# Spreading a side product over the first attention head of a graph network: earlier start, a split made in halves, and casts shared between two engines

## The chip, the cores and the metric

The kernel runs on one core of one Trainium2 chip. The metric is the time of one execution on the device in microseconds (us); lower is better. Three runs of the kernel before gave 1754.12, 1755.75 and 1757.56 us, so its median is 1755.75 us. One further execution was taken by the hardware profiler. The engines are TensorE (PE; its weight loads are listed apart as PEld), VectorE (DVE), ScalarE (ACT), GpSimd (POOL) and SyncE (SP), which only issues transfers here. ScalarE issues some transfers too.

## The reference: what is computed

Four residual layers of a graph network act on x (2708 nodes, 512 features) and one adjacency matrix of zeros and ones. Each takes h = relu(layernorm(x)) and adds its result to x. Layer 2, in which the change lies, is attention with 8 heads of 64 features:

```
Wh   = h @ W[head]                         # 2708 x 64
e    = leaky_relu(f1[n] + f2[m], 0.2)      # f1 = Wh . a1,  f2 = Wh . a2
e    = where(adj[n, m] > 0, e, -9e15)
out  = elu(softmax(e, over m) @ Wh)
```

The other layers multiply h with the adjacency (layer 0), with the first 64 neighbours of each node (layer 1), and with the neighbour mean and two dense products (layer 3).

## The kernel before

The nodes are cut into 22 chunks of 128; the last has 20. The layers run one after the other, with the edges of each overlapped: the first chunks of a layer start while the last of the layer before are still being summed. The neighbour pattern is held in SBUF for the whole kernel as uint8 tiles, `vT0` to `vT5`.

**Layer 2, projection stage.** `stages2` runs over the 22 chunks: load, normalize, transpose on TensorE, evict with relu on ScalarE (`hT`, line 247), multiply with all heads' weights (`wh_ps`, line 187), copy to SBUF on ScalarE (`wh`), store to DRAM (`whd`). VectorE and GpSimd multiply with a1 and a2 and reduce (`wh_a`, `f`), which gives `f12`, the values f1 and f2 of every node and head. From `f12` ScalarE makes exponentials: `er` of f1 (`exps_nodes`), `ef` and `ec` of f2 (`exps2`). `row2` turns a chunk of `er` into a row on TensorE, copies it on ScalarE and sends it to DRAM (`rT`), from where `load_row1` spreads it over all partitions (`rb`). In this way exp(leaky_relu(f1 + f2)) becomes the maximum of two products; common factors of a node cancel in the softmax.

**Layer 2, attention.** Work is listed in `steps`: ten units with 22 steps each, one step for each chunk m. The first head is two half-width units (1408 and 1300 columns), heads 1 to 6 are one full-width unit each (2708 columns), and the last head is two halves again. In one step:

- `scale` (line 1042) multiplies the 64 columns of Wh by `ef` on ScalarE, and in some steps also a constant column (`one6`), giving the weights `whs` (four buffers).
- `make` (line 1056) computes on VectorE, in one pass, max(rb, ec) times the pattern: the tile `t` (four buffers).
- `multiply` (line 1274) runs `t` past the weights on TensorE, in four column groups side by side: `av` collects the weighted sums of Wh, `sums` the sum of weights.
- In heads 1 to 6 and for the 17 chunks in `BY_SIDE`, `sums` is not formed from `t`. There `compare` (line 1077) makes a comparison mask on ScalarE by a very steep sigmoid with bias `eb`, and `multiply_sides` multiplies this with `parts`.

`parts` holds `ef` and `ec*ef`, each as three bf16 numbers that add up to the fp32 value. `split` (line 1313) makes them: a ScalarE cast to bf16, a VectorE subtraction giving the remainder (`rest`), and so on; it also makes `eb` and copies the last three parts in another order to `parts2`.

**The neighbour sums.** For heads 1 to 6 the comparison gives only one of two sums; to complete the other the kernel needs, once for all heads, the plain neighbour sum of the `ec*ef` parts. These are the `adj_sums`: 17 sets, one for each chunk in `BY_SIDE`. A set is four casts of a quarter of a pattern row from uint8 to bf16 (`mask`, line 1347, ScalarE, 704 or 650 columns) and eight matmuls with `parts2` (`count_neighbors`, line 1355). The casts go to buffers of the tag "x", of which there are five. They run within the first head, whose `sums` come from `t` and need no mask.

**The last chunk.** Its 20 rows of heads 1 to 6 are packed together as one 120-row tile (`tails_row`, `tails_w`, `tails_f`): `load_tails` issues their transfers, `exp_tails` and `make_tails` compute on them.

**What sets the order.** The loop over `steps` emits, at step s, `scale` and `make` for step s+3, `compare` for s+1, the matmuls for s, and then whatever `behind(step, function, ...)` has planned for s (the `behind` calls start at line 1397). A scheduler then orders each engine's instructions by its own estimate of readiness; `tc.issue_after(ins)` holds instructions of an engine behind `ins` if they are on the same engine. `made` lists the VectorE instruction of each step's `t`. The engines work through their lists in order, and semaphores carry data between them.

Of the kernel before, what the change touches and what calls it, by code (L numbers as in the profile page):

```python
# [8 lines left out]
F32 = mybir.dt.float32  # L9
F32R = mybir.dt.float32r  # L10
BF16 = mybir.dt.bfloat16
# [3 lines left out]
AF = mybir.ActivationFunctionType  # L15
ALU = mybir.AluOpType
# [4 lines left out]
P = 128  # L21

R = 128
# [21 lines left out]
def fast_layers(  # L45
# [36 lines left out]
    nc = tc.nc  # L82
    N, D = x_in.shape
    H, _, O = w2.shape
    NC = -(-N // R)
# [6 lines left out]
    def rows(c):  # L92
        return min(R, N - c * R)
# [18 lines left out]
    EARLY = NC // 2  # L112
# [10 lines left out]
    common = ctx.enter_context(tc.tile_pool(name="common", bufs=2))  # L123
# [146 lines left out]
    def dense(src, product_of, twice=True, more=(), scalar=False, rows_of=natural):  # L270

        kept = {}

        def size(c):
            return R if twice else rows(c)

        def load(c):
            kept[c] = load_x(src, c, twice=twice, rows_of=rows_of)

        def normalize(c):  # L280
            kept[c] = kept[c], norm(kept[c], size(c), scalar)

        def transpose(c):
            kept[c] = kept[c][0], relu_T(kept[c][1], size(c))

        def multiply(c):
            product_of(c, *kept.pop(c), size(c))

        return (0, load), (1, normalize), (2, transpose), (3, multiply), *more
# [113 lines left out]
    vT = []  # L403
# [69 lines left out]
    with ExitStack() as ring_ctx:  # L473
# [31 lines left out]
        with tc.tile_pool(name="l0", bufs=2) as wk, ExitStack() as ctx_l0:  # L505
            units = [(g, m) for g in range(len(groups)) for m in range(NC)]
            tiles, acc, sums, xs = {}, {}, {}, {}
# [190 lines left out]
            def first_dense(lag, fn):  # L698
                return lag, lambda i: fn(i) if i < NC else None
# [39 lines left out]
            first = [first_dense(lag, fn) for lag, fn in dense(x_in, product0, rows_of=paired)]  # L739
# [158 lines left out]
        def before1(c):  # L898
# [9 lines left out]
            lambda *args: product2(*args),  # L908
            False,
            [(3, lambda c: save_last2(c)), (4, lambda c: sums2(c)), (6, lambda c: rows2(c))],  # L910
            scalar=True,
        )
# [11 lines left out]
    BY_SIDE = [m for m in range(NC - 1) if m % 5 != 2]  # L924


    STEEP = 2.0**62
    ABOVE = 1.0 + 2.0**-21
# [9 lines left out]
    def in_tails(u, m):  # L938
        return m == NC - 1 and units[u][0] in middle
# [7 lines left out]
    def by_side(u, m):  # L947
        return 1 < u < len(units) - 1 and m in BY_SIDE
# [12 lines left out]
    ef = at.tile([R, NC, H], F32, name="ef")  # L961
    ec = at.tile([R, NC, H], F32, name="ec")
    eb = at.tile([R, NC, H], F32, name="eb")
    parts = at.tile([R, NC * H * 8 + S], BF16, name="parts")
    nc.gpsimd.memset(parts, 0.0)
    parts_of = parts[:, : NC * H * 8].rearrange("p (m h k) -> p m h k", h=H, k=8)

    parts2 = at.tile([R, len(BY_SIDE), 2, H, 3], BF16, name="parts2")
    nc.gpsimd.memset(parts2, 0.0)
    one6 = at.tile([R, S], F32, name="one6")  # L970
    nc.gpsimd.memset(one6, 0.0)
    nc.gpsimd.memset(one6[:, 6:7], 1.0)
    row, weight, wh, whs, acc, sides, made = {}, {}, {}, {}, {}, {}, []

    def load_row1(h, lo, hi):

        if lo == 0:
            row[h] = at.tile([R, N], F32, name="rb", bufs=2)
        src = rT[h : h + 1, lo:hi]
        nc.sync.dma_start(  # L980
            row[h][:, lo:hi],
            bass.AP(tensor=src.tensor, offset=src.offset, ap=[[0, R], [1, hi - lo]]),
        )
# [58 lines left out]
    def scale(s):  # L1042

        u, m = steps[s]
        h, q = units[u][0], rows(m)
        if in_tails(u, m):
            whs[s] = tails_w[:LINES, middle.index(h)]
            return
        t = at.tile([R, O + S], F32, name="whs", bufs=4)
        by = ef[:q, m, h : h + 1]  # L1050
        nc.scalar.activation(t[:q, :O], wh.pop((u, m))[:q], AF.Copy, scale=by)  # L1051
        if not by_side(u, m):
            nc.scalar.activation(t[:q, O:], one6[:q], AF.Copy, scale=by)
        whs[s] = t[:q]

    def make(s):
# [84 lines left out]
    def row2(c):  # L1141
        pf = ps.tile([P, R], F32, name="f_ps", tag="ps")
        nc.tensor.transpose(pf[:H], er[:, c], ident[:R, :R])
        r = at.tile([H, R], F32, name="row", bufs=2)
        nc.scalar.copy(r, pf[:H])
        nc.scalar.dma_start(rT[:, c * R : (c + 1) * R], r)

    def exps_nodes(cs):
        nc.scalar.activation(er[:, cs], f12[:R, cs, :H], AF.Exp, scale=1.0 - SLOPE2)

    def exps2(cs):
        nc.scalar.activation(ef[:, cs], f12[:R, cs, H:], AF.Exp)
        nc.scalar.activation(ec[:, cs], f12[:R, cs, H:], AF.Exp, scale=SLOPE2 - 1.0)


    LATE = NC - 5
    early_rows = [(0, EARLY // 2 + 1), (EARLY // 2 + 1, EARLY)]

    def rows2(c):
        for first, end in early_rows:  # L1160
            if c == end - 1:
                exps_nodes(slice(first, end))
            for n in range(2):
                if first <= first + 2 * (c - end + 1) + n < end and c >= end - 1:
                    row2(first + 2 * (c - end + 1) + n)
        if c == EARLY + 1:
            load_row1(*units[0])

        if c == LATE:
            exps2(slice(0, EARLY))  # L1170
            load_wh(0)
            load_wh(GROUP)
        if LATE < c <= LATE + 3:
            scale(len(made))
            make(len(made))

    def save_last2(c):
# [7 lines left out]
    tails = tails_ctx.enter_context(  # L1185
        tc.tile_pool(name="tails", bufs=1, side="right", reuse_waits="tile")
    )
# [122 lines left out]
                    t[j * step : j * step + height, : b - a],  # L1310
                )

    def split():

        nc.scalar.mul(eb, ec, -STEEP * ABOVE)
        rest = common.tile([P, D], F32, name="rest", tag="t", bufs=3)
        rest = rest[:R, : NC * H].rearrange("p (m h) -> p m h", h=H)
        for i in range(2):
            e = ef
            if i:  # L1320
                nc.vector.tensor_tensor(rest, ec, ef, ALU.mult)
                e = rest
            for k in range(3):
                part = parts_of[:, :, :, 3 * i + k]
                nc.scalar.copy(part, e)
                if k < 2:
                    nc.vector.tensor_tensor(rest, e, part, ALU.subtract)
                    e = rest
        for i, heads in enumerate((slice(1, H), slice(1, H - 1))):
            kinds = sorted({m % 5 for m in BY_SIDE})  # L1330
            for r in kinds:
                ms = [m for m in BY_SIDE if m % 5 == r]
                src = parts_of[:, r : ms[-1] + 1 : 5, heads, 3:6]
                at_i = [BY_SIDE.index(m) for m in ms]
                assert at_i == list(range(at_i[0], at_i[-1] + 1, len(kinds)))
                nc.scalar.copy(
                    parts2[:, at_i[0] : at_i[-1] + 1 : len(kinds), i, heads], src
                )


    fourths = [0, cut // 2, cut, (cut + N) // 2, N]
    counted, masks = [], {}

# [3 lines left out]
    def mask(i, j):  # L1347
        m = BY_SIDE[i]
        q = rows(m)
        g, k = where[m]  # L1350
        own = slice(fourths[j], fourths[j + 1])
        t = masks[i, j] = common.tile([P, D], F32, name="x", bufs=XBUFS).bitcast(BF16)
        nc.scalar.copy(t[:q, : own.stop - own.start], vT[g][:q, k, own])

    def count_neighbors(i):
        m = BY_SIDE[i]
# [37 lines left out]
    def behind(s, fn, *args):  # L1394
        plan.setdefault(s, []).append((fn, args))
# [3 lines left out]
    for c in range(EARLY, NC):  # L1399
        behind(4 + (c - EARLY) // 2, row2, c)  # L1400
    behind(10, load_row1, *units[1])
    behind(9, split)
    behind(12, load_tails)
    behind(18, exp_tails)
    behind(22, make_tails)
    behind(30, load_l3_weights)
    behind(30, spread_nodes)
    for u in range(2, len(units)):
# [3 lines left out]
        behind((u + 1) * NC - 1, evict, u, 0)  # L1412
        behind(min((u + 1) * NC, len(steps) - 1), evict, u, 1)
    for i in range(len(BY_SIDE)):
        first = 11 + 7 * i // 4
        for j in range(4):
            behind(first + j // 2, mask, i, j)
        behind(first + 2, count_neighbors, i)
# [17 lines left out]
    for s in range(len(steps)):  # L1436
        if s == (len(units) - 3) * NC + 1:
            tails_ctx.close()
            e3_ctx = ctx.enter_context(ExitStack())
            e3 = e3_ctx.enter_context(  # L1440
                tc.tile_pool(name="e3", bufs=2, side="right", reuse_waits="tile")
            )
        if s + 6 < len(steps) and (s + 6) % NC % GROUP == 0:
            load_wh(s + 6)
        if s + 3 < len(steps):
            scale(s + 3)
            make(s + 3)
        if s + 1 < len(steps):
            compare(s + 1)
        multiply(s)  # L1450
        multiply_sides(s - 1)
        for fn, args in plan.pop(s, ()):
            if fn in (load_l3_weights, spread_nodes, split):
                with tc.issue_after(made[s]):
                    fn(*args)
            else:
                fn(*args)
# [742 lines left out]
```

## Time and profile before

| | us |
|---|---|
| median of three runs | 1755.75 |
| the profiled execution, whole | 1757.88 |
| its span, from the first to the last instruction | 1756.1 |
| TensorE busy (98% of the span) | 1728.0 |
| VectorE busy (74%) | 1307.0 |
| ScalarE busy (48%) | 850.1 |
| first matmul of the attention | 812.56 |
| first matmul of the second half-unit of head 0 | 872.24 |
| first product of head 1 on VectorE | 907.28 |
| first matmul on the packed tail (end of head 0) | 912.51 |

The clock granted to TensorE was 0.994 in the mean. The shares in the table are averages over stages with different limits. In the projection stage and in the first head TensorE's matmuls carry the chain of work that ended last; from about 1081 us on, VectorE's products `t` carry it up to the end of the attention. In the answers below a line begins with its start and its length in us, or with engine and tile; "x16" is a count of instructions, and "[6.45 <-PE sums L1266]" says that the engine was idle for 6.45 us before and what ended this. One fp32 matmul of the program is two in the trace, and names lose their digits: `t2` of the code is `t`, `parts2` is `parts`, and a cast of the neighbour sums writes `x`.

### The profile page before, as it was taken

To read this page: it belongs to the slowest core of one execution; us is meant where nothing else is said; L and a number is where in the kernel's file an instruction comes from. 1 tells how busy PE (TensorE), PEld (TensorE's weight loads), DVE (VectorE), ACT (ScalarE), POOL (GpSimd) and SP (SyncE) were. 2 spreads that over 40 slices of the span, in tenths; PEclk is the share of its full clock that TensorE was granted. 3 is DMA by queue.
4 is the path that set the end of the run, shared out by engine and by line. 5 is a ranking of instruction groups with operands and counts; after the bars stand their busy time and mean duration, and the time that the engine had idled before them with its cause. 6 is when DMAs were issued, how large, how long until landed. Compare 5 with 4: busy or idle time off the path is not lost.

```text
span 1756.1 us, 29494 instructions
## 1 busy us (share of the span) xinstructions
PE 1728.0 (98%) x11280; PEld 1050.8 (60%) x11280; DVE 1307.0 (74%) x1889; ACT 850.1 (48%) x1547; POOL 248.0 (14%) x252
## 2 busy tenths in 40 slices
PE   8999999999999999999999999999999999999998
PEld 5567777744468887644474554433434455588886
DVE  7759889855455557878699999999999777633334
ACT  5447777622210000365888888888794566400000
POOL 1003323311111112265000000000001222100000
PEclk9999999999999999999899999999999999999999
DMA  8436666444551112332420221122022444313221
GB/s 291 139 117 199 206 207 186 136 114 129 115 135 49 48 49 66 113 126 93 125 63 15 60 64 34 38 64 61 14 68 69 135 139 132 112 34 110 74 72 41
DMA packets 167227, 177.37 MB, mean 101 GB/s; under 512 B 84127, under 2 KB 106591, under 8 KB 166060
## 3 DMA queue, kind: packets, MB, share of 16 engines
q1 hardware_dynamic: 144428, 131.99, 27.1%
q10 hardware_dynamic: 18808, 33.37, 5.1%
q0 software_dynamic: 3840, 10.03, 1.5%
q8 instruction: 90, 1.47, 0.4%
q14 instruction: 61, 0.50, 0.1%
HBM read 111.64 MB, written 55.36 MB: 95 GB/s over the span
## 4 chain that ended last, share of the span: by engine, by line
PE 84%; DVE 9%; issue 2%; ACT 2%; DMA 1%; SPq 0%; POOL 0%; ACTq 0%; DVEq 0%; POOLq 0%
PE acc L424 36%; PE av L1266 15%; PE nb_ps L187 8%; DVE t L1066 6%; PE h_ps L187 4%; PE line_ps L187 4%; PE sums L1266 4%; PE self_ps L187 4%; PE hT_ps L245 2%; PE wh_ps L187 2%; PE fused_ps L370 2%; PE av_ps L1219 1%; PE adj_sums L1365 1%; ACT b L1084 1%; DVE kt L870 0%
## 5 line engine op out<-in xcount | busy, mean ns | idle before, releaser
L1066 DVE SCALAR_TENSOR_TENSOR t<-rb,ec,vT 128x2708 f32<-128x2708 f32 (+2 forms) x214 | 510.7, 2453 | 19.5 <-PE sums L1266 17.8
L1266 PE MATMUL av<-t,whs 128*32 128x451 f32 (+5 forms) x4432 | 431.1, 514 | 4.4 <-DVE t L1066 1.4
L424 PE MATMUL acc<-halves,kt 128*128 128x512 f32 x1848 | 426.4, 391 | 2.4 <-DVE kt L870 2.1
L424 PEld LDWEIGHTS acc<-halves,kt 128*128 128x128 f32 x1848 | 345.2, 188 | 79.8 <-DVE kt L870 6.8
L1084 ACT ACTIVATE b<-t,eb 128x2708 bf16<-128x2708 f32 (+1 forms) x119 | 285.0, 2395 | 36.6 <-DVE t L1066 36.2
L1266 PEld LDWEIGHTS av<-t,whs 128*32 128x32 f32 (+1 forms) x4432 | 168.1, 110 | 182.2 <-issue 145.4
L424 PE MATMUL acc<-halves,ar 128*128 128x512 f32 x924 | 243.6, 414 | 0.0
L424 PEld LDWEIGHTS acc<-halves,ar 128*128 128x128 f32 x924 | 172.6, 188 | 58.2 <-issue 20.8
L223 ACT ACTIVATE ln_rs<-ln_mv,eps 128x1 f32<-128x1 f32 x88 | 25.6, 294 | 306.4 <-DVE ln_mv L221 298.4
L870 DVE SCALAR_TENSOR_TENSOR kt<-lastr,index,vT 128x512 fp32r<-128x512 int16 (+3 forms) x154 | 112.6, 742 | 75.8 <-PE acc L424 75.4
L1517 DVE CAST kt<-vT 128x512 fp32r<-128x512 uint8 (+3 forms) x154 | 56.3, 368 | 131.2 <-PE acc L424 131.2
L1233 POOL TENSOR_SCALAR z<-y 128x512 f32<-128x512 f32 x22 | 44.1, 2003 | 647.1 <-DMA aT<-avT 522.8
L555 DVE TENSOR_TENSOR_SCAN cum<-ai,deg 128x512 int16<-128x512 int32 (+2 forms) x110 | 128.3, 1170 | 0.0
L598 ACT ACTIVATE cum<-cum,limit 128x512 int16<-128x512 int16 (+3 forms) x132 | 88.0, 667 | 51.9 <-DVE deg L563 49.7
L1051 ACT ACTIVATE whs<-wh,ef 128x64 f32<-128x64 f32 x214 | 72.7, 343 | 54.3 <-PE sums L1266 22.0
L219 DVE BATCH_NORM_STATS2 ln_st<-x 128x6 f32<-128x512 f32 x88 | 60.3, 687 | 47.7 <-DMA x<-x 33.3
L1266 PE MATMUL sums<-t,whs 128*32 128x325 f32 (+4 forms) x952 | 92.8, 451 | 0.0
L187 PE MATMUL nb_ps<-wfn,hT 128*128 128x512 f32 x168 | 78.1, 609 | 2.1 <-ACT hT L247 2.1
L187 PE MATMUL h_ps<-w0s,hT 128*128 128x512 f32 x168 | 76.5, 598 | 0.0
L187 PE MATMUL wh_ps<-w2s,hT 128*128 128x512 f32 x168 | 75.9, 594 | 0.3 <-ACT hT L247 0.3
L549 ACT ACTIVATE ar<-ai 128x512 fp32r<-128x512 int32 (+2 forms) x132 | 75.0, 568 | 1.5 <-DMA ai<-in_adj 1.0
L187 PE MATMUL nb_ps<-wn,hT 128*128 128x512 f32 x168 | 75.6, 592 | 0.0
(210 smaller groups left out, 1908.2 us busy)
## 6 DMA issues: line engine op xcount, KB each, us to landing
x<-x SPq DMA_DIRECT2D x105, 256.0 KB
ai<-in_adj SPq DMA_DIRECT2D x84, 256.0 KB
x<-x ACTq DMA_DIRECT2D x84, 256.0 KB
x<-in_x SPq DMA_DIRECT2D x42, 256.0 KB
rb<-rT SPq DMA_DIRECT2D x7, 1354.0 KB
wh<-whd SPq DMA_DIRECT2D x63, 96.0 KB
packed<-two POOLq DMA_DIRECT2D x44, 128.0 KB, 3.2
whd<-wh SPq DMA_DIRECT2D x21, 256.0 KB
```

The lines of the kernel that those rows point to most:

```text
L187: nc.tensor.matmul(po[:n], lhsT[:, f, :n], w[:, f, :], start=(f == 0), stop=(f == NF - 1))
L219: nc.vector.bn_stats(st[:n], xc[:n])
L424: nc.tensor.matmul(acc[:R], weight[:, k * R : (k + 1) * R], parts[:, i, :], start=(m == 0 and i == 0), stop=(m == NC - 1),)
L549: nc.scalar.activation(ar[:, :gw], ai[:, :gw], AF.Square, accum_out=squares[:R, m, g : g + 1])
L555: nc.vector.tensor_tensor_scan(cum[:n, :gw], ai[:n, :gw], ai[:n, :gw], 0.0 if g == 0 else deg[:n, m : m + 1], op0=ALU.add, op1=ALU.max,)
L598: nc.scalar.activation(cum[:n, :gw], cum[:n, :gw], AF.Sign, bias=limit[:n], scale=-1.0, accum_out=signs[:n, m, g : g + 1],)
L870: nc.vector.scalar_tensor_tensor(by_chunk(kt, cs), lastr[:, cs[0] * R : (cs[-1] + 1) * R].rearrange("p (c r) -> p c r", r=R), index[:R, m ...
L1051: nc.scalar.activation(t[:q, :O], wh.pop((u, m))[:q], AF.Copy, scale=by)
L1066: ins = nc.vector.scalar_tensor_tensor(t[:q, : hi - lo], row[h][:q, lo:hi], ec[:q, m, h : h + 1], vT[g][:q, k, lo:hi], op0=ALU.max, op1=AL ...
L1084: nc.scalar.activation(b[:q, : hi - lo], weight[s][:, : hi - lo], AF.Sigmoid, bias=eb[:q, m, h : h + 1], scale=STEEP,)
L1266: nc.tensor.matmul(p[j * S : (j + 1) * S, : b - a], lhsT, rhs[:, part * size + a : part * size + b], start=(s % NC == 0), stop=(s % NC == ...
L1517: nc.vector.tensor_copy(by_chunk(kt, cs), pattern(m, cs))
```

## The change

- The neighbour sums are planned from step 1 on, over 40 steps (`first = 1 + 39 * i // 16`), where before they were planned from step 11 on, over 29.
- `split` becomes a function of a range of chunks. The first half (11 chunks) is made in the projection stage, at its chunk `EARLY + 1`; its exponentials (`exps2`) move up to chunk `EARLY - 1`, from `LATE`. The second half is made at step 9, where the whole was made before.
- Of the last eight sets (chunks from `EARLY` on), the fourth cast runs on VectorE and goes to a new tile `mask` with two buffers in the pool of the tails.
- A cast is held behind the scaling of step s+2 on ScalarE and behind the product of step s on VectorE.
- `exp_tails` moves from step 18 to 30, `make_tails` from 22 to 36.

```diff
+    def split(first, end):
+        cs = slice(first, end)
+        nc.scalar.mul(eb[:, cs], ec[:, cs], -STEEP * ABOVE)
+        rest = common.tile([P, D], F32, name="rest", tag="t", bufs=3)
+        rest = rest[:R, : (end - first) * H].rearrange("p (m h) -> p m h", h=H)
+        for i in range(2):
+            e = ef[:, cs]
+            if i:
+                nc.vector.tensor_tensor(rest, ec[:, cs], e, ALU.mult)
+                e = rest
+            for k in range(3):
+                part = parts_of[:, cs, :, 3 * i + k]
+                nc.scalar.copy(part, e)
+                if k < 2:
+                    nc.vector.tensor_tensor(rest, e, part, ALU.subtract)
+                    e = rest
+        for i, heads in enumerate((slice(1, H), slice(1, H - 1))):
+            kinds = sorted({m % 5 for m in BY_SIDE})
+            for r in kinds:
+                ms = [m for m in BY_SIDE if m % 5 == r and first <= m < end]
...
+                nc.scalar.copy(
+                    parts2[:, at_i[0] : at_i[-1] + 1 : len(kinds), i, heads], src
+                )
...
+        if c == EARLY - 1:
+            exps2(slice(0, EARLY))
         if c == EARLY + 1:
             load_row1(*units[0])
+            split(0, EARLY)

         if c == LATE:
-            exps2(slice(0, EARLY))
             load_wh(0)
...
         own = slice(fourths[j], fourths[j + 1])
+        n = own.stop - own.start
+        if j == 3 and m >= EARLY:
+            t = masks[i, j] = tails.tile([P, fourths[1]], BF16, name="mask", bufs=2)
+            nc.vector.tensor_copy(t[:q, :n], vT[g][:q, k, own])
+            return
         t = masks[i, j] = common.tile([P, D], F32, name="x", bufs=XBUFS).bitcast(BF16)
-        nc.scalar.copy(t[:q, : own.stop - own.start], vT[g][:q, k, own])
+        nc.scalar.copy(t[:q, :n], vT[g][:q, k, own])
...
-    behind(9, split)
+    behind(9, split, EARLY, NC)
     behind(12, load_tails)
-    behind(18, exp_tails)
-    behind(22, make_tails)
+    behind(30, exp_tails)
+    behind(36, make_tails)
...
     for i in range(len(BY_SIDE)):
-        first = 11 + 7 * i // 4
+        first = 1 + 39 * i // 16
         for j in range(4):
             behind(first + j // 2, mask, i, j)
         behind(first + 2, count_neighbors, i)
...
             if fn in (load_l3_weights, spread_nodes, split):
                 with tc.issue_after(made[s]):
                     fn(*args)
+            elif fn is mask:
+                with tc.issue_after(scaled[s + 2]), tc.issue_after(made[s]):
+                    fn(*args)
```

`scaled[s]` is the last ScalarE instruction of `scale` for step s. The whole `split` of before, with the same body over all 22 chunks, is removed.

More of the change, by code (lines that the diff above doesn't have):

```diff
@@ L972, in fast_layers @@
     nc.gpsimd.memset(one6[:, 6:7], 1.0)
-    row, weight, wh, whs, acc, sides, made = {}, {}, {}, {}, {}, {}, []
+    row, weight, wh, whs, acc, sides, made, scaled = {}, {}, {}, {}, {}, {}, [], {}
     def load_row1(h, lo, hi):
@@ L1050, in scale @@
         by = ef[:q, m, h : h + 1]
-        nc.scalar.activation(t[:q, :O], wh.pop((u, m))[:q], AF.Copy, scale=by)
+        ins = nc.scalar.activation(t[:q, :O], wh.pop((u, m))[:q], AF.Copy, scale=by)
         if not by_side(u, m):
-            nc.scalar.activation(t[:q, O:], one6[:q], AF.Copy, scale=by)
+            ins = nc.scalar.activation(t[:q, O:], one6[:q], AF.Copy, scale=by)
+        scaled[s] = ins.ins
         whs[s] = t[:q]
@@ L1153, in exps2 @@
         nc.scalar.activation(ec[:, cs], f12[:R, cs, H:], AF.Exp, scale=SLOPE2 - 1.0)
+    def split(first, end):
[18 more added lines that the diff above has]
+                ms = [m for m in BY_SIDE if m % 5 == r and first <= m < end]
+                src = parts_of[:, ms[0] : ms[-1] + 1 : 5, heads, 3:6]
+                at_i = [BY_SIDE.index(m) for m in ms]
+                assert at_i == list(range(at_i[0], at_i[-1] + 1, len(kinds)))
+                nc.scalar.copy(
+                    parts2[:, at_i[0] : at_i[-1] + 1 : len(kinds), i, heads], src
+                )
     LATE = NC - 5
@@ L1311, in evict @@
                 )
[L1313 to L1338, printed above, removed]
     fourths = [0, cut // 2, cut, (cut + N) // 2, N]
```

## The prediction

> **What bounds the kernel now.** I read the chain that ended last, then waits and the timeline around its first-head part. The first head (two half-width units of 22 steps, 812.56 to 912.51 us) is TensorE's. First the two products that pace it (start, length, line), then its largest hole, then VectorE:
>
> ```profile
> 836.47 1.37 PE L1266 MATMUL av<-t,whs 128*32 128x352 f32 x16
> 838.24 1.37 PE L1266 MATMUL av<-t,whs 128*32 128x352 f32 x16
> ...
> 866.75 5.95 PE L1365 MATMUL adj_sums<-x,parts 128*24 128x325 bf16 x18 [0.43 <-ACT x L1353]
> ...
> 865.95 5.99 ACT L1353 CAST x<-vT 128x650 bf16<-128x650 uint8 x9
> ...
> 874.51 9.79 DVE L1066 SCALAR_TENSOR_TENSOR t<-rb,ec,vT 128x1300 f32<-128x1300 f32 x6 [6.45 <-PE sums L1266]
> ...
> 907.28 203.66 DVE L1066 SCALAR_TENSOR_TENSOR t<-rb,ec,vT 128x2708 f32<-128x2708 f32 x69 [0.36 <-PE sums L1266]
> ```
>
> A 1408-wide step is 1.77 us of TensorE, a 1300-wide one 1.645 (875.82 to 877.46). In the hole the neighbour sums run one cast at a time (0.665 us each on ScalarE) and VectorE idles 6.45 us. From 907.28 VectorE never pauses: the waits from 905 to 1320 show 0.7 us for it, and 2708 columns come every 2.95 us. So the attention's end moves with the start T of the second head's first product, now 907.28. Four product buffers tie T to TensorE: that product takes the buffer of step 40 (step 41 starts at 906.88). The waits of 812 to 913:
>
> ```profile
> PE adj_sums L1365 <- ACT x L1353: 4.0, 8, 1.1
> PE av L1266 <- DVE f L1132: 1.2, 1, 1.2
> PE adj_sums L1365 <- ACT parts L1336: 1.0, 2, 0.8
> ...
> DVE t L1066 <- PE sums L1266: 17.8, 15, 6.4
> DVE f L1130 <- POOL wh_a L1119: 0.8, 1, 0.8
> ```
>
> VectorE thus idles 18.8 us before T. Two stretches (us, then busy PE, PEld, DVE, ACT, POOL, granted clock, DMA) show what the waits leave out, half clock after a hole:
>
> ```profile
> 850.00:852.00 2.00, 2.00 (x20) 1.14 (x15) 0.70 (x1) 1.68 (x5) 0.00 (x0) 0.50 0.77 116
> 868.00:870.00 2.00, 2.00 (x7) 0.29 (x6) 0.07 (x1) 2.00 (x5) 0.00 (x0) 0.50 0.57 132
> ```
>
> TensorE's sum: 22 x 1.77 + 22 x 1.645 = 75.1; eleven row transposes 2.5 (steps with two are 2.22 apart, so 0.225 each); 17 neighbour sets at 0.28 (853.35 to 853.63) = 4.8; 82.4 of the 99.95. Of the 17.5 lost, 7.8 is the bunch (8.83 from 863.41 to 872.24, less 1.05 for its 30 matmuls), 1.2 VectorE's f at 820.3, 1.0 the parts at 842, some 1.8 single casts at 845 to 848, 1.7 half clock at 848.5 to 851.8, 0.6 at 897; the rest is scattered.
>
> **What the skill says.** "TensorE: Matmul & The Clock Gate", Part 1, halves the clock after an idle window of about 3.4 us; the trace agrees (0.50 at 850, for about 3.3 us), though here windows with some work already trigger it. "VectorE: DVE Perf Modes", What auto-detection actually checks, lets a one-source copy inside SBUF take two elements a cycle. The trace agrees for uint8 to fp32:
>
> ```profile
> L1517 DVE CAST kt<-vT 128x512 fp32r<-128x512 uint8 x88 | 37.3, 425 | 98.2 <-PE acc L424 98.2
> L1517 DVE CAST kt<-vT 128x128 fp32r<-128x128 uint8 x22 | 4.8, 225 | 4.8 <-PE acc L424 4.8
> L1353 ACT CAST x<-vT 128x704 bf16<-128x704 uint8 x34 | 25.6, 771 | 1.1 <-PE adj_sums L1365 1.1
> ```
>
> 200 ns over 384 columns is 0.52 ns a column, so 650 columns take 0.50 us, 0.45 in a stream (products overlap by some 0.08: 3036 ns long, 2.95 apart). Output in bf16 is not shown; at one element a cycle it would be about 0.8. Either is near the 0.66 that the same cast takes on ScalarE.
>
> **The change, part by part.**
> *Sums spread.* Sets begin at step 3 and come every two or three steps; no more bunch. Same matmuls, 4.8 us. TensorE without waits would free step 40 at 812.56 + 1.2 + 38.9 + 19 x 1.645 + 2.5 + 16 x 0.28 = 890.9: gain 16.4.
>
> *Eight casts to VectorE.* 8 x 0.45 = 3.6 us (at 0.8: 6.4). VectorE's floor for T: 907.28 less 18.8, plus the 0.8 at GpSimd which stays, plus 3.6, less about 0.5 (five split operations of 176 columns, 0.41 each, become five of 88, taken as 0.32) = 892.4. Its two extra buffers let a set's fourth cast ignore the five-buffer ring.
>
> *Split in halves.* The first half moves into the projection stage: on ScalarE eb 0.3, six part casts (176 columns: 0.48 apart; 88 strided columns not shown, between 0.25 and 0.48, taken 0.32) and eight copies of about 0.16 (eight in 842.33 to 843.63) = 3.5 us. Out of that stage go three of five early casts (2.0) and one table load (1.28, moved to 817 to 821, where ScalarE now waits 4.1 us for f12): net +0.2. That stage is TensorE's, 3.88 us a chunk; hT is done 0.5 us before it is needed at 787.64, the tightest, later 1.8 and 2.9. VectorE's five extra operations (1.6) fit where it is busy 2.2, 1.9 and 1.8 of 4 us (784 to 796). The last early row copy slips behind parts copies, up to 0.9, and the first row load waits for it. I charge 0.5; a hand-over that misses would cost up to 3.
>
> *ScalarE in the first half-unit* is the new limit: 32 casts x 0.655 = 21.0; 19 scaling pairs x 0.46 (872.32 to 872.77) = 8.7; eleven rows with DMA issues x 0.5 (two in 824.20 to 825.22) = 5.7; second half of the split 3.3; exps 0.5; tails 1.0; 40.2 us. 2.9 of it runs before the wait for f12 ends at 821.4, so ScalarE ends at 858.7 if it never waits, TensorE at 857.5 (812.56 + 1.2 + 38.9 + 2.5 + 8.5 x 0.28). Both full, each waiting for the other through five cast buffers. In the second half-unit of before ScalarE was as full (per two steps 4 x 0.655 + 2 x 0.46 = 3.54 of 3.57 us) and TensorE lost 1.8 us. With the split's round trips I take twice that: 3.5, so the half-unit ends at 861.0.
>
> *Second half-unit.* ScalarE has 26 casts, 28 us of 38: slack. TensorE frees step 40 at 861.0 + 31.3 + 7.5 x 0.28 = 894.4. VectorE starts three steps ahead, about 855.1, and has 22 x 1.49 + 2.95 (tails) + 3.6 = 39.3: 894.4 too. Two equal chains which hand over at 0.35 us a wait: +2.1, T = 896.5, gain 10.8.
>
> *Moved loads and tails.* On SP two first-head loads slip past four tail DMAs each (2.9 us); they serve steps 15 and 18, over 8 us later: nothing. Tail exponentials move behind casts, their product stays four steps into the second half-unit. Second-half row load: last row now issued at 841.0, load at 843.9; needed near 855, so 5 us late would be free.
>
> *Second head's start.* ScalarE now does a 2.5 us sigmoid before the eight copies (0.44) that free the two sum banks: free at T + 2.95 + 2.5 + 3.6 = T + 9.05, wanted near T + 8.2. Step 45 ends near T + 12.0; VectorE wants its buffer at T + 11.8. I charge 0.4. After that all order is the same.
>
> Sum: 10.8 - 0.5 - 0.4 = 9.9 us. The profiled execution took 1757.88 (span 1756.1), so 1748.0; its runs' median is 2.1 lower, 1755.75, so **1745.9**.
>
> **Rivals.**
> - *Smaller gain, ScalarE decides.* If each of the nine sets in the first half-unit costs TensorE another 0.5 us, and a hole brings a half-clock window (1.7), T is 6.2 later: gain 3.7, 1752.0. For it: 40.2 us in 37 to 46. Against: sets are 2.5 steps apart, not bunched.
> - *Better: floors reached.* T = 892.4, gain 14.9 less 0.9: 1741.8. Against: three engines near full.
> - *No change.* The gain reappears as TensorE-bound middle heads. Against: over five steps TensorE needs 13.7 us (938.40 to 952.09), VectorE 14.75; only some loss within 3.5 us of zero could come.
> - *Slower: the first split stalls the projection.* Part casts on ScalarE wait for VectorE's remainder, which stands behind a wh_a that waits for ScalarE's own wh copy; hT stands behind the casts. If each of five round trips takes a whole chunk, 5 x 3.9 = 19.5 us against 10.8: near 1764. It decides once TensorE loses over 2.2 us in each of five chunks. Against: VectorE is half idle there, and hT has up to 2.9 us.
>
> **How the numbers follow.** Forecast 0.72, better 0.06, smaller 0.10 (all faster), no change 0.05, slower 0.07. Within 0.2% (3.5 us) is about what measurement can't tell from no change: faster 0.88, same 0.05, slower 0.07. The forecast's own range is 1743 to 1750 (casts at 0.8 add 2.8; part casts at 0.48 add 0.8; a half-clock window 1.7). For 8 in 10 I take 1741 to 1752, which takes in both faster rivals.
>
> **What would show it.** T near 896.5 and VectorE unbroken after it; no bunch of neighbour matmuls; VectorE's wait for PE sums down from 17.8 to some 6; ScalarE nearly full from 821 to 860 with small cast waits on TensorE; the VectorE cast near 0.50 us; the first attention matmul within 1 us of 812.56. Wrong if that matmul is over 2 us late, if the clock drops repeatedly before 860, or if VectorE pauses between 900 and 1300.

## The result: half to two thirds of the forecast gain, and from another edit than the one it was put down to

| | us |
|---|---|
| kernel before, median of nine executions | 1756.6 (1754.12 to 1757.95) |
| changed kernel, median of nine | 1752.01 (1749.58 to 1754.19) |
| ratio, 95% interval | 0.9972, 0.9962 to 0.9983 |
| forecast | 1745.9, range 1741 to 1752 |
| the changed kernel measured again beside experiments | 1750.21, ratio 0.9968 (0.9957 to 0.9979) |

The change makes the kernel faster by 4.6 us, by 6.2 in the second measurement; forecast were 9.9. The profiled execution took 1754.19 us with a span of 1752.3 (before: 1757.88 and 1756.1).

The prediction hung on T, the start of the second head's first product on VectorE: 907.28 before, forecast 896.5. The timeline of VectorE in the changed kernel (start, length, what it is, idle time before it and what ended that):

```profile
897.04 3.20 DVE L1067 SCALAR_TENSOR_TENSOR t<-rb,ec,vT 128x1300 f32<-128x1300 f32 x2
900.60 11.89 DVE L1067 SCALAR_TENSOR_TENSOR t<-rb,ec,vT 128x2708 f32<-128x2708 f32 x4 [0.36 <-PE sums L1297]
913.28 23.71 DVE L1067 SCALAR_TENSOR_TENSOR t<-rb,ec,vT 128x2708 f32<-128x2708 f32 x8 [0.79 <-PE av L1297]
```

T is 900.60, and VectorE then pauses once more, for 0.79 us, at its fifth product. The waits from 812 to 913 us, and the group of the new casts:

```profile
DVE t L1067 <- PE sums L1297: 6.2, 9, 1.9
PE av L1297 <- DVE t L1067: 2.7, 1, 2.7
PE adj_sums L1373 <- ACT x L1361: 1.9, 3, 1.1
DVE rest L1172 <- ACT parts L1170: 1.0, 1, 1.0
```

```profile
L1358 DVE CAST mask<-vT 128x650 bf16<-128x650 uint8 x8 | 4.0, 494 | 0.0
```

VectorE's wait for TensorE fell from 17.8 to 6.2, and the cast is as fast as forecast. TensorE's timeline shows its holes in that stretch:

```profile
824.24 1.93 PE L1297 MATMUL av<-t,whs 128*32 128x352 f32 x16 [2.66 <-DVE t L1067]
842.87 0.44 PE L1373 MATMUL adj_sums<-x,parts 128*24 128x325 bf16 x5 [1.15 <-ACT x L1361]
848.25 0.30 PE L1373 MATMUL adj_sums<-x,parts 128*24 128x325 bf16 x1 [0.62 <-ACT x L1361]
866.45 1.30 PE L1297 MATMUL av<-t,whs 128*32 128x325 f32 x16 [0.42 <-ACT whs L1051]
```

The bunch (8.8 us at 863 to 872 before) is gone. New is a hole of 2.66 us at step 4, where the kernel before waited 1.17, and half clock after it. In the stretches below, the columns are length, busy time of PE, PEld, DVE, ACT and POOL, then granted clock, DMA share and GB/s:

```profile
825.00:830.00 5.00, 5.00 (x47) 1.25 (x36) 5.00 (x4) 4.24 (x14) 0.00 (x0) 0.66 0.07 14
864.00:870.00 6.00, 5.41 (x76) 2.75 (x72) 5.47 (x3) 5.62 (x15) 0.00 (x0) 1.00 0.34 83
```

Executions do not all begin the attention at the same moment. So in what follows T is also counted from one fixed event, the start of the projection's matmuls of the chunk near 780 us (779.95 before, 780.34 in the changed kernel). From there T is 127.3 before and 120.3 in the changed kernel (119.1 in its second profile); the forecast is 896.5 - 779.95 = 116.55. Every T below is read from one profiled execution, and two of the changed kernel differ by 1.2, so a smaller difference in T shows little by itself.

### The profile page after: what moved, and what is told of

It is laid out like the page before. It is cut to its first block, busy times and chain, and to the rows that moved or that the text cites. A ratio compares the mean times of both kernels' runs of the same rounds, so it can differ in the third digit from the quotient of the medians.

```text
span 1752.3 us, 29486 instructions
## 1 busy us (share of the span) xinstructions
PE 1724.1 (98%) x11280; PEld 1078.8 (62%) x11280; DVE 1312.2 (75%) x1902; ACT 845.6 (48%) x1554; POOL 248.3 (14%) x252
## 4 chain that ended last, share of the span: by engine, by line
PE 86%; DVE 8%; ACT 2%; issue 2%; DMA 1%; SPq 1%; POOL 0%; ACTq 0%; DVEq 0%; POOLq 0%
PE acc L424 36%; PE av L1297 17%; PE nb_ps L187 8%; DVE t L1067 5%; PE sums L1297 4%; PE h_ps L187 4%; PE line_ps L187 4%; PE self_ps L187 4%; PE hT_ps L245 2%; PE fused_ps L370 2%; PE wh_ps L187 1%; DVE wh_a L1114 1%; PE av_ps L1250 1%; ACT b L1085 1%; DVE f L1131 1%
## 5 line engine op out<-in xcount | busy, mean ns | idle before, releaser
L1297 PE MATMUL av<-t,whs 128*32 128x451 f32 (+5 forms) x4432 | 445.5, 514 | 6.2 <-DVE t L1067 3.9
L1297 PEld LDWEIGHTS av<-t,whs 128*32 128x32 f32 (+1 forms) x4432 | 193.2, 110 | 167.9 <-issue 118.5
L1297 PE MATMUL sums<-t,whs 128*32 128x325 f32 (+4 forms) x952 | 104.4, 451 | 0.0
L1297 PE MATMUL sums<-b,parts 128*32 128x338 bf16 (+2 forms) x884 | 76.0, 308 | 0.0
```

What stands on the lines that cost most here:

```text
L1297: nc.tensor.matmul(p[j * S : (j + 1) * S, : b - a], lhsT, rhs[:, part * size + a : part * size + b], start=(s % NC == 0), stop=(s % NC == ...
```

## Experiments

Each was timed beside the kernel before on the same chip; ratios are to that. Diffs are to the kernel named.

**Is the early place of the first split half the loss?** The trace after suggested it. In the projection stage the last early row copy stands behind parts casts that wait for VectorE. Changed kernel, timelines of ScalarE, of SyncE's queue, and of VectorE:

```profile
788.87 0.58 ACT L1170 CAST parts<-rest 128x88 bf16<-128x88 f32 x1 [1.22 <-DVE rest L1172]
...
795.44 0.25 ACT L1146 COPY row<-f_ps 8x128 f32<-8x128 f32 x1
```

```profile
797.71 0.32 SPq L980 DMA_DIRECT2D rb<-rT  x1
```

```profile
802.02 1.69 DVE L1067 SCALAR_TENSOR_TENSOR t<-rb,ec,vT 128x1408 f32<-128x1408 f32 x1 [0.72 <-DMA rb<-rT]
...
822.52 1.67 DVE L1067 SCALAR_TENSOR_TENSOR t<-rb,ec,vT 128x1408 f32<-128x1408 f32 x1
```

Before, these stood at 792.40, 794.72, 799.10 and 819.61: all 2.9 to 3.0 earlier. From the first product to step 4's VectorE takes 20.5 us in both, with hardly a pause: it is full there, so a late row load is a late step 4. The first experiment moves that half behind the row copies:

```diff
         if c == EARLY + 1:
             load_row1(*units[0])
-            split(0, EARLY)
+        if c == EARLY + 3:
+            split(0, EARLY)
```

> The changed kernel, with the first half of the split emitted two chunks later (behind the last early row copy and the first row load). Theory A: that half, where the change puts it, holds up the last early row copy and with it the first row load and VectorE's whole chain of first products by 2.9 us, which TensorE pays as a late start (1.0), a 2.7 us hole at step 4 and half clock behind it (1.7). Then here the first product is back at about 799.2 us and step 4's at 819.7, the hole is 1.2 or less, TensorE has full clock at 825 to 830, T is about 897 and the time about 1748, some 4 us below the changed kernel. Theory B: the loss is ScalarE's, which is full in the first half-unit whatever the row load does: T stays at 900 and the time is 1751 to 1752.

Measured: 1749.11 us, ratio 0.9958 (0.9944 to 0.9971). The row copy is back, and with it the products:

```profile
791.98 0.25 ACT L1146 COPY row<-f_ps 8x128 f32<-8x128 f32 x1
```

```profile
819.57 1.66 DVE L1067 SCALAR_TENSOR_TENSOR t<-rb,ec,vT 128x1408 f32<-128x1408 f32 x1
...
898.60 11.89 DVE L1067 SCALAR_TENSOR_TENSOR t<-rb,ec,vT 128x2708 f32<-128x2708 f32 x4 [0.36 <-PE sums L1298]
```

The mechanism is shown, but the difference needed both kernels on one chip:

> The changed kernel itself, beside the next three on the same chip: 1751 to 1753.

> The same kernel as split_later, beside the changed kernel on one chip. If the early place of the split costs what its first run showed, it is 2 to 4 us below the changed kernel in the median; if that difference was scatter, it is within 1 us of it.

1750.21 (0.9968, 0.9957 to 0.9979) and 1749.9 (0.9960, 0.9947 to 0.9974). From the chunk near 780 us, T is 120.3 and 119.1 in the two profiles of the changed kernel, 119.3 and 118.6 in those of split_later. So the early place costs perhaps 0.7 us at T, less than the 1.2 between two profiles of one kernel, and 0.3 to 2.9 in the medians; the intervals overlap. A good part of TensorE's loss at step 4 is taken up again before T. This is not where 5 us went.

The same half alone, on the kernel before, with the changed kernel's function `split`:

```diff
+        if c == EARLY - 1:
+            exps2(slice(0, EARLY))
         if c == EARLY + 1:
             load_row1(*units[0])
+            split(0, EARLY)
...
         if c == LATE:
-            exps2(slice(0, EARLY))
...
-    behind(9, split)
+    behind(9, split, EARLY, NC)
```

> The kernel before, with the split in two halves as the change has it (first half and its exponentials in the projection stage), and nothing else of the change: sums from step 11 on as before, all casts on ScalarE, tails at their old steps. Theory A: the row load is 2.9 us late and TensorE pays up to 4.2 of it before step 11, of which up to 1.0 comes back at 842 us, where the kernel before waits for parts; T about 910, time about 1759.5, slower than the kernel before by some 3 us. Theory B: the late row load is taken up by later waits; the time is that of before, 1756 to 1757, or up to 1 us less.

1755.22, ratio 0.9993 (0.9985 to 1.0001). Theory A's time was wrong: the hole at step 4 is there (2.37 us), but the kernel before's waits for parts at 842 us and the half clock of 848 to 852 us are gone, and in the time the two about cancel. T is 125.2, 2.1 us earlier than before; of that the medians show 1.3, with an interval that takes in no change.

**Are the shared casts or the spacing the gain?** First the changed kernel without VectorE's casts:

```diff
-        if j == 3 and m >= EARLY:
-            t = masks[i, j] = tails.tile([P, fourths[1]], BF16, name="mask", bufs=2)
-            nc.vector.tensor_copy(t[:q, :n], vT[g][:q, k, own])
-            return
```

> The changed kernel, with every cast on ScalarE (VectorE's eight go back). My account: in the second half-unit the three engines are nearly level. TensorE needs 2.44 x 1.645 + 0.28 = 4.29 us for a set and its steps, ScalarE with all four casts 4 x 0.665 + 2.44 x 0.46 = 3.78, VectorE loses 3.3 us of work; so VectorE's load falls, TensorE stays the bound, and single casts come late again for 0 to 2 us: 1751 to 1754. Rival: only the shared casts keep ScalarE in time, and without them the wait for single casts returns: 1756 or more. Second rival: VectorE alone paces the second half-unit of the changed kernel (it never pauses from 867 to 900 us), and without its casts T falls by up to 3 us: 1749.

1751.48, 0.9973 (0.9966 to 0.9981), beside 0.9972 and 0.9968 for the changed kernel: no gain from the eight casts is shown in the time. VectorE waits 8.9 us for TensorE where it waited 6.2, so in good part its casts filled idle time. T is 121.5 against 120.3 and 119.1, so that a gain of 1 to 2 us may be hidden in the scatter. Then the kernel before with another spacing:

```diff
-        first = 11 + 7 * i // 4
+        first = 11 + 29 * i // 16
```

> The kernel before, with only the spacing changed: single split at step 9, first set at step 11 as before, the 17 sets spread evenly to step 40 (29 steps instead of 28 quarters of 7 that end at step 39 but bunch behind the tails), every cast on ScalarE. ScalarE then has 17 x 2.62 + 31 x 0.46 + 1.0 = 59.8 us of work from 843.6 us on, so T is about 903.5 and the time about 1753 if casts and products only wait on that sum. Rival: what the change gains comes from the early start of the sums, and a spacing from step 11 has the same bunch as before: 1756 or more.

1756.46, 1.0003 (0.9994 to 1.0011): nothing. This edit is small, since the sets of the kernel before were 1.75 steps apart already; the run shows that the bunch there isn't the plan's spacing. ScalarE's timeline still has nine casts in a row, as in the kernel before:

```profile
864.63 5.99 ACT L1353 CAST x<-vT 128x650 bf16<-128x650 uint8 x9
```

T is 124.4, earlier than before, but VectorE then pauses for 1.49 us at its fifth full product, and none of it arrives in the median.

**What is left at the second head's start, and in the first half-unit.** All three build on split_later.

```diff
-        first = 1 + 39 * i // 16
+        first = 1 + 36 * i // 16
```

> split_later, with the 17 sets spread over 36 steps instead of 39 (the last one is counted at step 39 instead of 42), so that ScalarE's eight copies of the neighbour sums stand ahead of the second head's first comparison instead of behind it. Theory: the 0.79 us pause at VectorE's fifth product of the second head is theirs, and goes: 0.8 us less than split_later, less what denser casts cost in the first half-unit (up to 0.5): 1748.0 to 1749. Rival: the pause has another cause (the products of the second head's tail step) and stays: split_later's time or up to 1 us more.

1749.56, 0.9959 (0.9946 to 0.9973). The pause is gone; T from the chunk near 780 us is 118.5. Timeline of VectorE:

```profile
899.02 38.44 DVE L1067 SCALAR_TENSOR_TENSOR t<-rb,ec,vT 128x2708 f32<-128x2708 f32 x13 [0.38 <-PE sums L1298]
```

So the pause was the sums' copies. Its 0.8 us can't be told from split_later_again in the medians.

```diff
-        if j == 3 and m >= EARLY:
+        if j == 3 and m < EARLY:
```

> split_later, with VectorE taking the fourth cast of the nine sets of the first half-unit instead of that of the eight of the second. Theory: ScalarE is the full engine of the first half-unit only; relieved there of 9 x 0.655 = 5.9 us, the waits for single casts (1.2 and 0.6 us) go, VectorE has the 3.7 us there that it now waits for TensorE, and the second half-unit does without sharing, as casts_on_scalar showed: T about 896.5, time about 1747.5. Rival: VectorE comes late in the first half-unit with 9 casts beside its products (its lead is gone at step 4 already): 1750 or more.

1749.55, 0.9961 (0.9947 to 0.9975). T is 117.5, 1 to 2 us better, but one set waited 3.7 us for VectorE's cast, as the rival had it, and the time is split_later's.

```diff
-        first = 1 + 39 * i // 16
+        first = 1 + 36 * i // 16
...
-        if j == 3 and m >= EARLY:
+        if j == 3 and 3 <= i < 14:
```

> split_later with the sets over 36 steps (as in later_last_set_sooner) and VectorE's share given to sets 4 to 14, in both half-units, not to the last eight: sets 1 to 3 stay on ScalarE, where later_first_half_shared waited 3.7 us for VectorE's first cast. Theory: no single-cast waits above 0.3 us in the first half-unit (2.9 us in split_later_again), no pause at the second head's fifth product; T some 1 us earlier than split_later's, measured from the same point of the projection, and 1748 to 1749. Rival: T is VectorE's sum by now, since its products and casts come from 867 to 900 us without a pause, and moving casts gives nothing: 1749.5 or more.

1750.68, 0.9968 (0.9955 to 0.9980), T 118.9: no gain. VectorE also waits inside its list for ScalarE's parts casts (1.2 and 1.9 us here, 1.0 in the changed kernel, none in the kernel before), since the second half of the split now runs among casts.

**Is the early start needed at all?** On the changed kernel, the single split at step 9 comes back, the sums start at step 11, and VectorE takes every fourth cast:

```diff
-        if c == EARLY - 1:
-            exps2(slice(0, EARLY))
         if c == EARLY + 1:
             load_row1(*units[0])
-            split(0, EARLY)
...
         if c == LATE:
+            exps2(slice(0, EARLY))
...
-    behind(9, split, EARLY, NC)
+    behind(9, split, 0, NC)
...
-        first = 1 + 39 * i // 16
+        first = 11 + 29 * i // 16
...
-        if j == 3 and m >= EARLY:
+        if j == 3:
```

> The changed kernel, with the single split at step 9 and the start at step 11 put back (17 sets over 29 steps), and VectorE taking the fourth cast of all 17 sets. It asks what carries the gain: casts_on_scalar kept it without sharing; this one keeps sharing without the early start. ScalarE's work from 843.6 us on falls from 59.8 by 17 x 0.655 to 48.7 us, so it would be done at 892; VectorE gets 17 x 0.41 = 7.0 us, which its 15 us of waiting in spread_alone holds; T about 899, no late row load, no hole at step 4 above 1.2: about 1750, as the changed kernel or up to 1 us less. Rival: the early start is what counts, since parts, tails and the second half-unit's row load still meet the sums between step 11 and 22 and the bunch at 863 us stays: 1754 or more.

1747.69, 0.9954 (0.9940 to 0.9967). VectorE's timeline has the head's last half-width product and the next head's first four in one line:

```profile
894.09 13.53 DVE L1067 SCALAR_TENSOR_TENSOR t<-rb,ec,vT 20x1300 f32<-20x1300 f32 x5
908.70 26.66 DVE L1067 SCALAR_TENSOR_TENSOR t<-rb,ec,vT 128x2708 f32<-128x2708 f32 x9 [1.08 <-PE av L1295]
```

Four full products take 11.89, so T is 894.09 + 13.53 - 11.89 = 895.7, or 116.6 from the chunk near 780 us: the forecast T, without the early start. (T is worked out in this way for spread_alone, late_start_unshared, 119.1, and late_start_eight_shared, 118.9, too.) Two relatives tell what does it. late_start_unshared:

```diff
-        if j == 3:
-            t = masks[i, j] = tails.tile([P, fourths[1]], BF16, name="mask", bufs=2)
-            nc.vector.tensor_copy(t[:q, :n], vT[g][:q, k, own])
-            return
```

late_start_eight_shared:

```diff
-        if j == 3:
+        if j == 3 and m >= EARLY:
```

> late_start_shared with every cast on ScalarE (single split at step 9, sets from step 11 over 29 steps, tails at steps 30 and 36, casts held behind their step's scalings as the change has it). It tells whether the 8.8 us between late_start_shared and spread_alone are the shared casts' or come from the other two edits that late_start_shared keeps. Theory (sharing): ScalarE has 59.8 us from 843.6 on against 48.7, so T is 903.5 or later and the time 1754 to 1757. Rival (tails and holding): 1749 to 1751.

> late_start_shared with only the last eight fourth casts on VectorE, as in the changed kernel. ScalarE's sum is 59.8 - 8 x 0.655 = 54.6, done at 898.2, TensorE's last set right behind: T about 899, time about 1750, the changed kernel's. If it is at 1747 to 1748 like late_start_shared, the early start and its price alone are what separates the changed kernel from it; if at 1753 or more, the early start is worth some 2 us for eight shared casts.

1751.22, 0.9971 (0.9961 to 0.9981), and 1749.49, 0.9965 (0.9953 to 0.9977); with 17 shared casts it was 1747.69. In the medians sharing gives 1.7 us for eight casts and 3.5 for seventeen here, at T 0.2 and 2.5; all three intervals overlap, so a gain is likely but not shown. But late_start_unshared is 5.2 us faster than spread_alone, and has only two edits more: later tail steps, and the rule that holds each cast behind a scaling. The program built from the kernel before with only the tails' steps moved has the same instructions in the same order on every engine. That left the rule.

**The rule alone, and everything but the rule.** held_alone is the kernel before with `scaled` and

```diff
+            elif fn is mask:
+                with tc.issue_after(scaled[s + 2]):
+                    fn(*args)
```

> The kernel before, with only the rule that a cast may not be ordered ahead of the scaling of its step + 2 on ScalarE; sums, split and tails where they were, every cast on ScalarE. Theory: the bunch of the kernel before is not the spacing of its sets (they are even already, 1.75 steps apart) but ScalarE's order: nine casts in a row (865.95 to 871.94) stand ahead of the scaling that TensorE's next step wants, and the tails' exponentials, drawn ahead of the last parts copies, wait 2.8 us for their loads. Held, the casts come two to four at a time, the tails' exponentials move behind them, and the time is 1751 to 1752, as late_start_unshared. Rival: the later tails steps are needed too (18 and 22 against 30 and 36): 1755 or more.

changed_not_held is the changed kernel without it, for both engines:

```diff
-            elif fn is mask:
-                with tc.issue_after(scaled[s + 2]), tc.issue_after(made[s]):
-                    fn(*args)
```

> The changed kernel without that rule. If holding the casts is what the change gains by, single casts run ahead of the scalings again and most of the 5 us is gone: 1754 to 1756. If the early start and the shared casts had an effect of their own, it stays within 1 us of the changed kernel: 1750 to 1753.

held_alone: 1752.01, 0.9970 (0.9958 to 0.9981). changed_not_held: 1758.01, 1.0008 (0.9999 to 1.0016). The timelines of VectorE have T, first with the rule alone, then without it:

```profile
901.96 35.49 DVE L1067 SCALAR_TENSOR_TENSOR t<-rb,ec,vT 128x2708 f32<-128x2708 f32 x12 [0.36 <-PE sums L1267]
...
906.32 11.89 DVE L1067 SCALAR_TENSOR_TENSOR t<-rb,ec,vT 128x2708 f32<-128x2708 f32 x4 [0.38 <-PE sums L1297]
```

The rule alone gives the changed kernel's gain; without it the rest of the change gives none (VectorE's casts, drawn ahead too, then wait 5.0 us for their buffers). The timeline of ScalarE shows why. The kernel before, at the turn of the half-units and, earlier, at its last parts:

```profile
840.62 0.20 ACT L1010 ACTIVATE tails_f<-tails_f 120x1 f32<-120x1 f32 x1 [2.84 <-DMA tails_f<-f]
...
865.95 5.99 ACT L1353 CAST x<-vT 128x650 bf16<-128x650 uint8 x9
871.84 0.59 ACT L1051 ACTIVATE whs<-wh,ef 128x64 f32<-128x64 f32 x2
```

The changed kernel without the rule:

```profile
864.89 8.75 ACT L1361 CAST x<-vT 128x704 bf16<-128x704 uint8 x13
873.54 0.59 ACT L1051 ACTIVATE whs<-wh,ef 128x64 f32<-128x64 f32 x2
```

The kernel before with the rule:

```profile
860.67 2.05 ACT L1354 CAST x<-vT 128x704 bf16<-128x704 uint8 x3 [0.50 <-PE adj_sums L1366]
862.62 0.79 ACT L1307 COPY out<-av 128x352 f32<-128x352 f32 x2
863.31 0.46 ACT L1307 COPY out<-sums 128x352 f32<-128x352 f32 x1
863.65 0.60 ACT L1051 ACTIVATE whs<-wh,ef 128x64 f32<-128x64 f32 x2
```

TensorE's next step needs the scaling `whs`. In the kernel before nine casts stand ahead of it in ScalarE's list, without the rule in the changed kernel thirteen; TensorE meanwhile gets one cast at a time to multiply. With the rule the scaling comes right behind the evictions. The tails' exponential, which held ScalarE for 2.84 us in front of the last parts copies, moves behind casts too, to 852.85, where its data is there. From the chunk near 780 us, T is 121.1 in held_alone and 126.8 in changed_not_held, near the 127.3 of before. In changed_not_held the tails' exponential comes late (856.06) and waits for nothing, too, yet T is hardly earlier; so the bunch looks like the greater part of what the rule removes, but no run takes it away alone.

**A version that beats both.** late_start_shared with the sets over 26 steps, so that the copies of the sums come before the second head's first comparison:

```diff
-        first = 11 + 29 * i // 16
+        first = 11 + 26 * i // 16
```

> late_start_shared with the 17 sets over 26 steps instead of 29, so that the copies of the sums come ahead of the second head's first comparison. The pause at VectorE's fifth product of the second head (1.08 us there) goes, as the 0.79 did in later_last_set_sooner; ScalarE's 48.7 us then stand against 26 steps, 46 us, so up to 1.5 us of single-cast waits come back: 1747 to 1748.5. Rival: the denser sets bunch again: 1749 or more.

1746.46 (1744.34 to 1746.76), 0.9942 (0.9929 to 0.9955). Waits from 812 to 913 us, where the kernel before had 17.8 for VectorE and 4.0 for single casts; the pause of 1.08 us is gone:

```profile
PE av L1295 <- DVE f L1133: 1.9, 1, 1.9
DVE t L1067 <- PE sums L1295: 1.8, 4, 0.8
PE adj_sums L1371 <- ACT x L1359: 1.6, 3, 0.8
```

It is 10.2 us faster than the kernel before in the medians beside it (1756.65). Against late_start_shared the 1.2 us lie within overlapping intervals.

## Why the prediction was wrong, step by step

Two steps failed. The size of the first half-unit was wrong: counted from the chunk near 780 us, T is 3.7 us later than forecast, of which 0.65 arose before the attention, 4.4 in the first half-unit, and 1.35 came back in the second. And the cause of the gain was wrong: it was put down to the earlier, wider spread of the sums, and it is the ordering rule's.

- *What bounds the kernel.* Right: the time followed T. After 1081 us the chain that ended last alternates between TensorE's matmuls and VectorE's products, in both kernels, so it isn't VectorE's alone; but from 905 us to the end of the attention VectorE's products waited for TensorE only 0.7 us before and 0.8 after. But T's gain doesn't arrive whole. Of 7.0 us (127.3 to 120.3) the pause took 0.8; the kernel before's profiled execution was also 1.3 us above its median of nine, and the two profiled executions differ at the layer's turn (last section).
- *Sums spread, no more bunch.* This step failed in its cause. The bunch went as forecast, but spread_alone shows that spreading from step 11 doesn't remove it, and changed_not_held that the early start and the shared casts don't either; held_alone shows that the rule does. The prediction quoted the nine casts in a row and read them as "one cast at a time". It listed no cost for the rule, although the diff has it, and so gave its gain to edits that, without the rule, bring none (changed_not_held).
- *Split in halves.* The charge of 0.5 was for a row copy up to 0.9 late. It is 1.7 to 2.7 late in the two profiles (counted from the chunk near 780 us), step 4's product 1.5 to 2.5; the hole of 2.66 and one half-clock window follow. Undone, it gives back some 0.7 at T, within the scatter. The rival named the right mechanism, casts on ScalarE waiting for VectorE's remainder, yet not the place: the row load behind them, not `hT`.
- *ScalarE in the first half-unit.* This term was too small. The forecast had 48.4 us from the first attention matmul to the second half-unit; it took 52.9 (813.60 to 866.45) and 52.3 in the second profile, 51.3 and 51.8 in split_later. The 3.5 us for waits were added to TensorE's end, 857.5, although ScalarE's own sum ended later, at 858.7. Nor was ScalarE "nearly full": it was busy for 31.1 of the 39 us from 821 to 860, the issuing of transfers not counted. The cast waits that the trace lists are 1.9, below the 3.5 charged. The rest is the hole, the half clock and small waits, some of them for rows. late_start_shared and late_start_unshared, which have 17 and 22 of ScalarE's casts in this half-unit where the changed kernel has 32, need 49.3 (811.77 to 861.04) and 49.2. So the early start lengthens it; whether by the number of casts or by their place among rows, parts and scalings isn't separated.
- *Second half-unit.* Right, a little cautious: 35.5 forecast, 34.15 measured (866.45 to 900.60).
- *Eight casts to VectorE.* Price right (0.49 long, 0.41 in the stream). In this plan casts_on_scalar shows no gain from them in the time.
- *Moved loads and tails: nothing.* The steps themselves, yes; but the tails' exponential had held up ScalarE in the kernel before. The prediction put that 1.0 us of TensorE down to the parts.
- *Second head's start.* 0.4 charged, 0.79 measured; mechanism as stated.
- *Sum.* 10.8 at T was possible, as late_start_shared shows with 10.7; the changed kernel reached 7.0 and 8.2. The time landed at the "smaller gain" rival, 1752.0, given 0.10. In part that is luck: its half-clock window came, but by the row load, not by the sets; its T was 6.2 later than forecast, where 3.7 and 2.5 were measured; and the second measurement is 1750.21.

Open is how the 2.5 to 3.7 us between the changed kernel's T and late_start_shared's divide between the early place (0.7), nine more shared casts (late_start_eight_shared has 118.9) and the waits of VectorE for parts; no single run isolates the last.

## What to carry to other kernels

Price every edit of a diff, the ordering rules first: a rule that only says what may not run ahead of what can be the whole gain, and a row of equal instructions in one engine's list is a question of what stands behind them. When a side job is moved earlier, ask whose in-order list it enters and which transfer is issued behind it. A neat agreement between a sum and a removed wait doesn't show which edit removes it; take each out on its own.

## What the runs showed of the hardware

Half clock came in whole windows of about 3.4 us, each costing up to 1.7. At the turn from layer 2 to layer 3, where TensorE works in pieces, there were one, two or three of them from execution to execution: in the seventeen profiles the half-clock stretch there lasted about 3.4 us in eight, 6.8 in eight and 10.2 in one. That one is the changed kernel's profiled execution (up to 5.1 us lost); that of the kernel before had two windows (3.4), changed_again one (1.7). Four stretches of the changed kernel, then its longest gap on TensorE ahead of the half clock:

```profile
1345.00:1350.00 5.00, 1.98 (x29) 0.92 (x26) 4.77 (x8) 2.74 (x3) 1.62 (x1) 1.00 0.08 30
1350.00:1355.00 5.00, 5.00 (x35) 2.23 (x35) 3.94 (x9) 2.50 (x5) 2.82 (x3) 0.56 0.52 135
1355.00:1360.00 5.00, 5.00 (x6) 2.09 (x7) 2.66 (x5) 3.17 (x5) 0.00 (x0) 0.50 0.45 135
1360.00:1365.00 5.00, 5.00 (x17) 2.47 (x15) 3.08 (x12) 2.06 (x3) 0.45 (x1) 0.91 0.56 151
...
1349.92 0.63 PE L245 MATMUL hT_ps<-ident,hn 128*128 128x128 f32 x4 [1.83 <-DVE hn L234]
```

Between the two profiled executions of the changed kernel, 1754.19 and 1749.45 us, the windows make up to 3.4 of the 4.7 us. That they are also behind the scatter of some 4 us between its other executions is likely, but not shown; it is a reason not to compare two single ones. In the stretch ahead of these windows TensorE was busy for 1.98 of 5 us with no gap above 1.83, so no whole window was idle. The Trainium skill ("TensorE: Matmul & The Clock Gate", Part 1, What's actually happening) ties half clock to at least one idle window of about 3.4 us; here it came without one, and the measurement decides.
